# Layer 3 of a four-layer image kernel: where y is summed, the order of the scans, the last chunks' taps, and the places of the first loads

## The chip, the cores and the metric

The kernel runs on one core of one Trainium2 chip. TensorE (PE) multiplies matrices, VectorE (DVE), ScalarE (ACT) and GpSimd (POOL) work on 128 partitions at a time, and SyncE (SP) issues most of the DMAs. The metric is the time of one execution on the device in microseconds (us); lower is better. Profile times count from the start of the span.

## The reference, cut to what matters

The input x is (4, 64, 64, 128) in fp32: four images of 64 x 64 pixels and 128 channels. Four layers follow each other: a 7 x 7 neighbourhood attention, a full attention over the 4096 pixels of an image, a gated product with a row sum and a layer norm, and a selective scan in four directions. The change is in the last of these, which is

```python
xz = x @ Win
xb, z = jnp.split(xz, 2, axis=-1)                 # 256 channels each
xb = silu(depthwise_conv_3x3(xb) + conv_b)
xf, xt = xb as (B, 256, L), and with rows and columns exchanged
xs = stack([xf, xf[..., ::-1], xt, xt[..., ::-1]], axis=1).reshape(B * K, 256, L)
x_dbl = einsum('bcl,cd->bdl', xs, Wxproj)         # 8 numbers for delta, one B, one C
dt_kb = x_dbl[:, :8].reshape(K, B, 8, L)
delta = softplus(einsum('kdr,kbrl->bkdl', dt_weight, dt_kb) + dt_bias)
h[l]  = exp(delta[l] * A) * h[l - 1] + delta[l] * u[l] * B[l]
y[l]  = h[l] * C[l] + D * u[l]
y = y0 + y1 reversed + y2 turned + y3 reversed and turned
yz = y * silu(z);  out = layernorm(yz) @ Wout
```

The reshape from (B * K) to (K, B) mixes images and directions. So sixteen sequences are scanned for each of two halves of 128 channels. Source image k supplies its four directions b = 0 to 3 to the outputs of the four images: the scan (k, b) is added to output image b, plainly for k = 0 and 1, and with rows and columns exchanged for k = 2 and 3.

## The kernel before, in words

**Layers 0 to 2** (`layers_0_to_2`) run image by image. Within `layer_1(b)` a loop of 32 steps holds PE's long stretches of matmuls (L586, L619); at each step `between(i)` puts in one part of layer 2 (`turn`, `mix`, `add`, `norm`, for chunk n of 512 pixels from i = 6 + 4n) and one part of layer 3's front (`front(b)`), which lags half an image: chunks 4 to 7 of an image are done in the next image's loop. For the last image there is no next loop, and `end(i)` does them at i = 30 to 41.

**Layer 3's front**, for a chunk n of image i: `load` brings back x3, which `norm` had stored in DRAM (x3_d); `project` (L744) multiplies it by Win into xh, a tile with halo rows, which POOL copies from chunk to chunk; `gate` (L772) makes silu(z); `begin`, `multiply`, `add_parts` and `add_taps` compute the nine convolution taps on ACT, POOL (L813) and DVE (L822); `activate` (L764) makes u; `lower` (L833) makes D u, the dt, B and C rows (stored in dbl_d), and `times_b` (L868) stores u times B in ub_d. D u of the images 2m and 2m + 1 (the odd one reversed) is summed in DRAM:

```python
if i & 1:
    nc.gpsimd.dma_start(du_d[i >> 1][f][:, L - hi:L - lo], du, accum_op=ALU.add)
else:
    nc.sync.dma_start(du_d[i >> 1][f][:, lo:hi], du)
```

**Layer 3's scan stage** (`layer_3`) goes through 64 steps of `todo`; a step is two scans (two directions) of 128 channels x 1024 pixels. f (the channel half) is the outermost loop, then source image k, then the directions 0, 1 and 2, 3, with four chunks each. A step consists of: `deltas` (PE multiplies dbl by dt, L1144; ACT softplus, L1152, into de; POOL multiplies by ub into inp, L1154), issued one step ahead; `decay` (ACT exp into h in PSUM, L1164); `back` (DVE scan, L1178, its last column kept by L1181, and its product with C). For even k the product is written straight into y in SBUF (L1194). For odd k it goes to yo, a ring of 4 buffers (L1189), a POOL DMA adds it to y in SBUF (L1190), and SP stores y into y_d (L1192) unless it is the last pair (f, k) = (1, 3), whose y stays in SBUF. The load of a 2 MB row of C, broadcast to 128 partitions (`load_c`), comes 16 times, that of ub (`load_ub`, two halves of 1 MB) 8 times.

D u comes in beside this: `load_z` (L1103) loads the sums, `add_z` (L1105) adds the turned one on DVE (L1106, in steps 2 and 3) and stores the result as z_d, and from step 4 on POOL DMAs add z_d to y (L1211), two after each step.

**Layer 3's output stage** adds y and the turned y (`yts`, loaded by `load_turned`), multiplies by the gate, takes the norm and multiplies by Wout, in 32 chunks of 512 pixels.

**Order.** `tc.keep_in_program_order` pins some instructions on their engine (ACT in the scan stage, the whole output stage); the rest is ordered by the scheduler within each engine's queue. A ring (`tag`, `bufs`) makes a new tile wait for the release of the oldest. D u, u, silu(z), the sums of taps and others share the ring c512 of 9 tiles; the tag "ring" has 5 places of 16 KB per partition. POOL's DMAs signal through eight semaphores in turn, and so do SP's: the ninth waits until the first has landed.

Of the kernel before, what the change touches and what calls it, by code (L numbers as in the profile page):

```python
# [67 lines left out]
RC = CH // W  # L68

# [7 lines left out]
def conv_seq(ctx, tc, x, mata, matb, cols, rows, rpb, dtw, convw, sel, out):  # L77
# [13 lines left out]

    ub_d, zf_d = stored("ub_d"), stored("zf_d")
    du_d = [[dram.tile([P, L], F32, name=f"du_d{i}_{f}") for f in range(2)] for i in range(2)]
# [3 lines left out]
    fronts = x3_d, ub_d, zf_d, du_d, dbl_d, ct_d, gw_d, bw_d  # L97
# [9 lines left out]

    layers_0_to_2(tc, xf, mata, matb, rows, rpb, convw, sel, ident, cl, dram, *fronts)
    layer_3(tc, of, dtw, ident, cl, dram, *fronts)


@with_exitstack
def layers_0_to_2(
    ctx, tc, xf, mata, matb, rows, rpb, convw, sel, ident, cl, dram, x3_d, ub_d, zf_d, du_d, dbl_d, ct_d, gw_d, bw_d
# [3 lines left out]
    big = ctx.enter_context(tc.tile_pool(name="big", bufs=1))  # L118
# [20 lines left out]
    once = big.tile([P, NMA - nma + NROW - nrow], F32, name="once", tag="ring", bufs=5)  # L139
# [11 lines left out]

    def ring(shape, name):

        return big.tile(shape, F32, name=name, tag="ring", bufs=5)
# [497 lines left out]

    def layer_2(b, xt):
# [47 lines left out]
        def norm(n):  # L701
            mv, rd = kept.pop(n)
            for k in range(4):
                x = xt[:, 4 * n + k, :]
                nc.vector.tensor_scalar(x, x, mv[:, k, 0:1], rd[:, k:k + 1], ALU.subtract, ALU.mult)
            x3 = tmp.tile([P, CH], F32, name="x3", tag="c512", bufs=9)
            transpose_tiles(
                xt, 4 * n, x3,
                lambda o, i: nc.vector.tensor_scalar(
                    in_blocks(o), by_block(i, "r b c"), cl("ln_s"), cl("ln_b"), ALU.mult, ALU.add  # L710
                ),
            )
            nc.sync.dma_start(x3_d[b][:, bass.ts(n, CH)], x3)
# [12 lines left out]
    def front(b):  # L726
# [9 lines left out]
        def load(i, n):  # L736
            x = x_of[i, n] = tmp.tile([P, CH], F32, name="xc", tag="g1")
            nc.sync.dma_start(x, x3_d[i][:, bass.ts(n, CH)])
# [49 lines left out]
        def taps(i, n):  # L788


            v = (1, 0) if n < NCH - 1 else (-1, 0)
            gp, ve = [v, (-1, 1), (1, -1), (1, 1)], [(-v[0], 0), (0, -1), (0, 1), (-1, -1)]
            return (gp[:2], ve + gp[2:]) if at_end(i, n) else (gp, ve)

        def multiply(i, n, f, which):
            for k in which:
                dy, dx = taps(i, n)[0][k]
# [10 lines left out]
        def add_parts():  # L808
            for i, n, f, k, p in parts_of:
                of = taps(i, n)[0]  # L810
# [8 lines left out]
        def add_taps(i, n, f):  # L819
            for dy, dx in taps(i, n)[1]:  # L820
                acc, x, c = tap(n, f, dy, dx)
                nc.vector.scalar_tensor_tensor(acc, x, c, acc, ALU.mult, ALU.add)  # L822

        def activate(i, n, apart=False):
            if apart:
                u_of[i, n] = [tmp.tile([P, CH], F32, name="u1", tag="c512", bufs=9) for _ in range(2)]
                for f in range(2):
                    silu(i, n, u_of[i, n][f], accs[n & 1][:, f, :])
# [4 lines left out]
        def lower(i, n):  # L833

            lo, hi = CH * n, CH * n + CH
            u = u_of[i, n]
            for f in range(2):
                du = tmp.tile([P, CH], F32, name="du", tag="c512", bufs=9)
                nc.scalar.activation(du[:, ::-1] if i & 1 else du, u[f], AF.Copy, scale=cl("d", 2 * i + f))
                if i & 1:  # L840
                    nc.gpsimd.dma_start(du_d[i >> 1][f][:, L - hi:L - lo], du, accum_op=ALU.add)
                else:
                    nc.sync.dma_start(du_d[i >> 1][f][:, lo:hi], du)
# [70 lines left out]
        def convolve(i, n, fs, half):  # L914
            for f in fs:
                if half == 0:
                    begin(n, f)
                multiply(i, n, f, range(len(taps(i, n)[0]))[2 * half:2 * half + 2])
# [3 lines left out]
        def end(i):  # L922

            c = B - 1
            for n, at in ((5, 30), (6, 34), (7, 38)):
                if i == at:
                    load(c, n)
                if i == at + 1:
                    project(c, n)
                    for k in (n - 1, n)[0:1 + (n == NCH - 1)]:  # L930
                        convolve(c, k, range(2), 0)
                        convolve(c, k, range(2), 1)
                if i == at + 2:
                    gate(c, n)
            for n, at in ((4, 34), (5, 37), (6, 41), (7, 41)):
                if i == at:
                    activate(c, n, True)
                    lower(c, n)

        def turn(i):  # L940
# [33 lines left out]
            if b == 0 and i == 3:  # L974
                output_weights()
            if b == B - 1:
# [42 lines left out]
def layer_3(ctx, tc, of, dtw, ident, cl, dram, x3_d, ub_d, zf_d, du_d, dbl_d, ct_d, gw_d, bw_d):  # L1019
    nc = tc.nc  # L1020
    def pool(name, bufs=1, **kw):
# [4 lines left out]

    y_d = [
        [[dram.tile([P, L], F32, name=f"{name}{b}_{f}") for f in range(2)] for b in range(B)] for name in ("yn_d", "yt_d")  # L1030
    ]
    z_d = [dram.tile([P, L], F32, name=f"z_d{f}") for f in range(2)]
    bc_d = [[dbl_d[b][RANK:RANK + 1, :], dbl_d[b][RANK + 1:RANK + 2, :], ct_d[b]] for b in range(B)]


    dbl = wp.tile([P, L], F32, name="dbl")
    dt = wp.tile([P, DI], F32, name="dt")
    nc.sync.dma_start(dt, dtw)

    na = wp.tile([P, 2 * B], F32, name="na")  # L1040
    nc.scalar.activation(na, cl("a_log", n=2 * B), AF.Exp)
    nc.vector.tensor_scalar(na, na, -1.0, None, ALU.mult)
    gw = wp.tile([P, 2, C], F32, name="gw")
    bw = wp.tile([P, C], F32, name="bw")
    eps = wp.tile([P, 1], F32, name="eps")
    nc.vector.memset(eps, 1e-5)

    def by_rows(t):
        return t.rearrange("p (i j) -> p i j", j=W)


    ct = wp.tile([W, 2, W], F32, name="ct")

    def turn_c(b, pt):
# [4 lines left out]

    ub_s, cb_s = [wp.tile([P, L], F32, name="ub_0")], [wp.tile([P, L], F32, name="cb_0")]  # L1060

    def load_ub(tile, f, k):
        for g in range(2):
            half = bass.ts(g, L // 2)
            nc.sync.dma_start(tile[:, half], ub_d[k][f][:, half])

    def load_c(tile, k, t):

        nc.sync.dma_start(tile, bc_d[k][1 + t][0].partition_broadcast(P))
# [11 lines left out]
    for b in range(B):  # L1081
        nc.sync.dma_start(dbl[32 * b:32 * b + NDBL, :], dbl_d[b])
        if b == 1:
            load_ub(ub_s[0], 0, 0)
            load_c(cb_s[0], 0, 0)
# [5 lines left out]
    SC = 2 * CH  # L1091
    NSC = L // SC
    yp = ctx.enter_context(pool("y"))
    ub_s.append(yp.tile([P, L], F32, name="ub_1"))
    cb_s.append(yp.tile([P, L], F32, name="cb_1"))
    ys = [yp.tile([P, L], F32, name=f"y{b}") for b in reversed(range(B))][::-1]

    zs, zt = ys[2:4], ub_s[1]  # L1100

    def load_z(f, part):
        nc.sync.dma_start(zt if part else zs[f], du_d[part][f])  # L1103

    def add_z(f):  # L1105
        nc.vector.tensor_tensor(turned(zs[f]), turned(zs[f]), by_rows(zt), ALU.add)  # L1106
        for g in range(4):
            quarter = bass.ts(g, L // 4)
            nc.sync.dma_start(z_d[f][:, quarter], zs[f][:, quarter])

    for f, part in ((0, 0), (0, 1), (1, 0)):
        load_z(f, part)
    nc.sync.dma_start(gw, gw_d)
    nc.sync.dma_start(bw, bw_d)
    nc.sync.dma_start(ct[:, 0, :], by_rows(bc_d[B - 1][1])[0])
    with pool("s", 2) as sp, pool("psC", 2, space=PSUM) as psp:

        todo = []  # L1120
        fks = [(f, k) for f in range(2) for k in range(B)]
        for j, (f, k) in enumerate(fks):
            for half in range(2):
                loads = []
                if half == (j == 0) and j + 1 < len(fks):
                    loads.append((load_ub, ub_s[(j + 1) % 2], *fks[j + 1]))
                i = 2 * j + half + 1
                if i < 2 * len(fks):
                    loads.append((load_c, cb_s[i % 2], fks[i // 2][1], i & 1))
                for at_n in range(NSC):  # L1130
                    n = NSC - 1 - at_n if k & 1 else at_n
                    todo.append((loads, [(f, k, 2 * half + q, n, ub_s[j % 2], cb_s[half]) for q in range(2)]))
# [5 lines left out]
        def deltas(pair):  # L1138

            pdt = [psp.tile([P, 2, CH], F32, name=f"pdt{j}", tag=f"dt{j}", bufs=1) for j in range(2)]  # L1140
            for g in range(2):
                for j, (f, k, b, n, _, _) in enumerate(pair):
# [6 lines left out]
            for j, (f, k, b, n, ub, _) in enumerate(pair):  # L1149
                kf = 2 * k + f  # L1150
                de = sp.tile([P, SC], F32, name="de", tag="de", bufs=5)
                act(nc.scalar.activation(de, pdt[j].rearrange("p g t -> p (g t)"), AF.Softplus, bias=cl("dt_b", kf)))  # L1152
                inp = sp.tile([P, SC], F32, name="inp", tag="inp", bufs=4)
                nc.gpsimd.tensor_tensor(  # L1154
                    by_rows(inp), by_rows(de), at(ub, b ^ (k & 1), SC * n, SC * n + SC), ALU.mult
# [13 lines left out]
        def back(f, k, b, n, ub, cb, inp, h):  # L1169
# [9 lines left out]
            if n != last:  # L1179
                ends[b] = sp.tile([P, 1], F32, name="end", tag="end", bufs=4)  # L1180
                nc.vector.tensor_copy(ends[b], h[:, 0:1] if k & 1 else h[:, SC - 1:SC])  # L1181
            c = (cb[:, ::-1] if order & 1 else cb)[:, lo:hi]
            flip = slice(None, None, -1) if b & 1 else slice(None)
            if b & 1:
                lo, hi = L - hi, L - lo
            y = ys[b][:, lo:hi]
            if k & 1:
                yo = sp.tile([P, SC], F32, name="yo", tag="yo", bufs=4)
                nc.vector.tensor_tensor(yo[:, flip], h, c, ALU.mult)  # L1189
                nc.gpsimd.dma_start(y, yo, accum_op=ALU.add)  # L1190
                if (f, k) != (1, 3):
                    nc.sync.dma_start(y_d[k >> 1][b][f][:, lo:hi], y)  # L1192
            else:
                nc.vector.tensor_tensor(y[:, flip], h, c, ALU.mult)  # L1194
                if b >> 1 == k >> 1:
                    late.append((y, z_d[f][:, lo:hi]))
# [3 lines left out]
        for j, ((loads, pair), after) in enumerate(zip(todo, todo[1:] + [None])):  # L1200
# [3 lines left out]
            hs = [decay(step, de) for step, (de, _) in zip(pair, parts)]  # L1204
            for step, (_, inp), h in zip(pair, parts, hs):
                back(*step, inp, h)

            for _ in range(2 if j > 3 else 0):
                if late:
                    y, z = late.pop(0)  # L1210
                    nc.gpsimd.dma_start(y, z, accum_op=ALU.add)  # L1211
# [222 lines left out]
```

## Time and profile before

| | us |
|---|---|
| median of 3 runs | 3858.29 |
| lowest, highest | 3853.61, 3859.43 |
| profiled execution: its own time | 3861.6 |
| profiled execution: span | 3859.8 |
| PE, DVE, ACT, POOL busy | 3378.9, 2806.5, 2705.7, 1443.5 |
| mean granted clock of TensorE | 0.903 |

The span runs from the first to the last instruction in the trace; the execution's own time is 1.8 us longer. In the lists of groups, `out<-in` names the tiles, then the shapes and the count; behind the bars stand the busy time, the mean of one in ns, and the idle time of the engine just before them with what ended it. In the chain, each row is start, length, and what ran. PE and PEld are TensorE's matmuls and weight loads; an fp32 matmul is recorded as two passes.

### The profile page before, as it was taken

What the parts mean: (1) busy time and instruction counts of PE and PEld (TensorE: products, weight loads), DVE (VectorE), ACT (ScalarE), POOL (GpSimd) and SP (SyncE); (2) the same over time, 40 slices, a digit from 0 to 9 for tenths busy, and PEclk for the clock granted to TensorE, in tenths of its full rate; (3) what the DMA queues carried; (4) which work ended last, traced back from release to release, by engine and by line L of the source; (5) the groups of instructions that cost most, each with busy time, mean ns of one, the idle gap of its engine ahead of it and who ended that gap; (6) DMA issues with size and microseconds to landing.
All of it is one profiled execution on the core that took longest, in us unless ns stands there. A gap on an engine that the chain in (4) does not pass through costs nothing.

```text
span 3859.8 us, 69106 instructions
## 1 busy us (share of the span) xinstructions
PE 3378.9 (88%) x26676; PEld 2778.6 (72%) x26676; DVE 2806.5 (73%) x4855; ACT 2705.7 (70%) x4391; POOL 1443.5 (37%) x1556
## 2 busy tenths in 40 slices
PE   6999999999999999999999999999999944665647
PEld 4679989966799999668999995689999821222236
DVE  2667777856677878566778875667787848998968
ACT  3865667767677767676777676767776846998934
POOL 5510022244122222441223224412222346888866
PEclk7999999999999999999999999999999955555579
DMA  5100000121010112210111022100011176998998
GB/s 138 46 3 25 12 18 29 54 91 34 17 48 29 37 35 59 85 34 17 48 31 40 29 72 75 31 17 26 31 41 31 51 209 211 271 282 260 258 285 274
DMA packets 192525, 326.61 MB, mean 85 GB/s; under 512 B 22175, under 2 KB 110780, under 8 KB 185500
## 3 DMA queue, kind: packets, MB, share of 16 engines
q1 hardware_dynamic: 152900, 253.29, 19.1%
q0 software_dynamic: 19776, 60.17, 8.4%
q10 hardware_dynamic: 19520, 8.73, 0.8%
q8 instruction: 210, 3.44, 0.4%
q14 instruction: 119, 0.97, 0.1%
HBM read 178.17 MB, written 110.47 MB: 75 GB/s over the span
## 4 chain that ended last, share of the span: by engine, by line
PE 52%; DVE 20%; ACT 11%; issue 7%; DMA 6%; POOL 4%; SPq 1%; DVEq 0%; POOLq 0%; ACTq 0%
PE po L619 16%; PE sc L586 16%; DVE mx L598 4%; PE pt L470 3%; DVE mx L593 2%; POOL inp L1154 2%; PE sc L435 2%; PE po L481 2%; DVE acc L822 2%; DMA y<-yo 2%; DVE h L1178 2%; ACT pr L453 2%; ACT st L589 2%; ACT st L613 1%; PE pz L772 1%
## 5 line engine op out<-in xcount | busy, mean ns | idle before, releaser
L619 PE MATMUL po<-v,st 128*128 128x129 f32 x8192 | 1084.0, 275 | 4.1 <-ACT st L613 4.1
L586 PE MATMUL sc<-qT,kT 128*128 128x128 f32 x8192 | 1080.5, 276 | 0.4 <-ACT st L589 0.4
L586 PEld LDWEIGHTS sc<-qT,kT 128*128 128x128 f32 x8192 | 1001.0, 192 | 21.4 <-issue 18.6
L619 PEld LDWEIGHTS po<-v,st 128*128 128x128 f32 x8192 | 999.0, 192 | 5.8 <-issue 5.8
L589 ACT COPY st<-sc 128x512 f32<-128x512 f32 x1024 | 576.0, 583 | 496.9 <-PE sc L586 490.4
L612 DVE TENSOR_TENSOR st<-st,pb 128x2048 f32<-128x2048 f32 x256 | 574.0, 2283 | 46.9 <-PE pb L609 46.8
L613 ACT ACTIVATE st<-st 128x2048 f32<-128x2048 f32 x256 | 482.8, 1908 | 10.8 <-DVE st L612 9.3
L593 DVE TENSOR_TENSOR mx<-mx,st 128x1024 f32<-128x1024 f32 x256 | 314.2, 1227 | 235.5 <-ACT st L589 233.0
L1144 PE MATMUL pdt<-dbl,dt 8*128 8x512 f32 x512 | 308.5, 1088 | 194.6 <-ACT de L1152 186.4
L1154 POOL TENSOR_TENSOR inp<-de,ub 128x1024 f32<-128x1024 f32 x128 | 363.8, 2996 | 87.0 <-ACT de L1152 57.3
L1144 PEld LDWEIGHTS pdt<-dbl,dt 8*128 8x128 f32 x512 | 115.8, 314 | 384.6 <-ACT de L1152 314.4
L461 POOL TENSOR_SCALAR pr<-pr,sm 128x308 f32<-128x308 f32 (+3 forms) x512 | 243.4, 494 | 264.8 <-DVE sm L459 196.2
L681 POOL TENSOR_TENSOR x<-x,row 128x512 f32<-128x512 f32 x32 | 50.2, 1568 | 686.0 <-PE pt L253 686.0
L813 POOL TENSOR_TENSOR gsum<-gsum,tp 128x504 f32<-128x504 f32 (+1 forms) x176 | 246.0, 1399 | 152.5 <-ACT gsum L801 83.4
L453 ACT ACTIVATE pr<-pr,mx 128x308 f32<-128x308 f32 (+3 forms) x512 | 262.5, 517 | 0.0
L598 DVE TENSOR_TENSOR mx<-mx 128x512 f32<-128x512 f32 (+2 forms) x384 | 237.7, 619 | 6.0
L822 DVE SCALAR_TENSOR_TENSOR acc<-xh,cc,acc 128x504 f32<-128x504 f32 (+3 forms) x272 | 217.3, 832 | 17.8 <-ACT acc L786 16.9
L1178 DVE TENSOR_TENSOR_SCAN h<-h,end,inp 128x1024 f32<-128x1024 f32 x96 | 220.8, 2345 | 6.4 <-ACT h L1164 3.9
L470 PE MATMUL pt<-ident,pr 128*88 128x128 f32 (+5 forms) x1472 | 205.7, 277 | 7.8 <-ACT prT L472 7.8
L439 DVE CUSTOM_DVE_ANT_0 pr<-sc,bias_m 128x266 f32<-128x266 f32 (+1 forms) x384 | 151.7, 451 | 69.0 <-PE sc L435 65.3
L470 PEld LDWEIGHTS pt<-ident,pr 128*88 128x88 f32 (+5 forms) x1472 | 165.0, 139 | 45.5 <-ACT prT L472 31.6
L472 ACT COPY prT<-pt 110x512 f32<-110x512 f32 (+3 forms) x240 | 138.9, 579 | 77.8 <-PE pt L470 77.8
(225 smaller groups left out, 5230.4 us busy)
## 6 DMA issues: line engine op xcount, KB each, us to landing
y<-yo POOLq DMA_DIRECT2D x64, 512.0 KB, 12.6
zf_d<-zf SPq DMA_DIRECT2D x64, 256.0 KB
ub_d<-u SPq DMA_DIRECT2D x64, 256.0 KB
cb<-ct_d SPq DMA_DIRECT2D x8, 2048.0 KB
ub<-ub_d SPq DMA_DIRECT2D x16, 1024.0 KB
cb<-dbl_d SPq DMA_DIRECT2D x8, 2048.0 KB
y<-z_d POOLq DMA_DIRECT2D x32, 512.0 KB, 14.4
yn_d<-y SPq DMA_DIRECT2D x32, 512.0 KB
```

Of the source, the lines that this page charges most:

```text
L453: pin(nc.scalar.activation(k.pr[:, h], k.pr[:, h], AF.Exp, bias=k.mx[:, h:h + 1], accum_out=k.sm[:, h:h + 1]))
L470: pin(nc.tensor.transpose(pt[0:n, h, :], k.pr[:, h, at:at + n], ident))
L586: nc.tensor.matmul(ps[:, r, :], lhsT=kT[:, bass.ts(G * g + r, P)], rhs=qT[:, bass.ts(i, P)], start=True, stop=True)
L589: nc.scalar.copy(k.st[:, G * g:G * g + G, :], ps)
L593: nc.vector.tensor_tensor(k.mx, k.mx, k.st[:, 4 * g - 4:4 * g + 4, :], ALU.max)
L598: nc.vector.tensor_tensor(mx[:, 0:n, :], mx[:, 0:n, :], mx[:, n:2 * n, :], ALU.max)
L612: nc.vector.tensor_tensor(part, part, pb.unsqueeze(1).to_broadcast([P, 16, P]), ALU.add)
L613: nc.scalar.activation(part, part, AF.Exp)
L619: nc.tensor.matmul(k.po, lhsT=k.st[:, j, :], rhs=v[:, j, :], start=(j == 0), stop=(j == NT - 1))
L1144: nc.tensor.matmul(pdt[j][:, g, :], lhsT=dt[o:o + RANK, P * f:P * f + P], rhs=at(dbl[o:o + RANK, :], k & 2, g0, g0 + CH), start=True, stop ...
L1154: nc.gpsimd.tensor_tensor(by_rows(inp), by_rows(de), at(ub, b ^ (k & 1), SC * n, SC * n + SC), ALU.mult)
L1178: nc.vector.tensor_tensor_scan(h[:, way], h[:, way], inp[:, way], prev, ALU.mult, ALU.add)
```

## The change

1. **D u.** y_d becomes a set of DRAM tiles of 128 x 1024, for both halves f, both forms t (plain, turned) and all four images. `lower` writes D u straight into the four that it belongs to, by SP stores for even images and by POOL DMAs that add for odd ones: eight DMAs of 256 KB a chunk instead of two. `load_z`, `add_z`, z_d, du_d and L1211 are gone.
2. **y.** Every product of a scan goes through yo (ring of 6 instead of 4; de has 4 instead of 5) and is added by a POOL DMA: into y_d in DRAM, or, for (f, k) = (1, 3), into y in SBUF. For (f, k) = (1, 2) the product is written to y in SBUF, and the DRAM tile is added to it later, one DMA in each following step. The 48 stores of y are gone.
3. **Order of the scans.** k is the outermost loop; within it the parts are (f one, directions 0 and 1), (two, 0 and 1), (two, 2 and 3), (one, 2 and 3). A row of C then serves both halves, so there are 8 such loads instead of 16.
4. **Last image, chunks 4 to 7.** x3 stays in SBUF (x3k), without store and reload. The nine taps become nine TensorE matmuls into PSUM for each half f, with diagonal matrices of the coefficients, which POOL makes at i = 6 of the last image. The steps of `end` lie at other i.
5. **First loads.** dbl of images 0 and 1, ub and the row of C for the first steps are loaded at i = 32 of the last image, into the places of layer 1's qT and of the ring; y, the second row of C and others also take over layer 1's places. dt and na are made at the start of the kernel.
6. **Output.** The turned y is loaded in four pieces of 512 KB per image instead of two of 1 MB, and `yts` has another order.

```diff
+    na = const.tile([P, 2 * B], F32, name="na")
+    nc.scalar.activation(na, cl("a_log", n=2 * B), AF.Exp)
...
-            x3 = tmp.tile([P, CH], F32, name="x3", tag="c512", bufs=9)
+            stays = b == B - 1 and n >= 4
+            if stays:
+                x3 = fresh[n] = tmp.tile([P, CH], F32, name="x3k", tag="g1")
+            else:
+                x3 = tmp.tile([P, CH], F32, name="x3", tag="c512", bufs=9)
...
-            nc.sync.dma_start(x3_d[b][:, bass.ts(n, CH)], x3)
+            if not stays:
+                nc.sync.dma_start(x3_d[b][:, bass.ts(n, CH)], x3)
...
+        def diagonals():
+            dg = x_of["dg"] = ring([P, 2, 9, P], "dg")
+            for f in range(2):
+                for t in range(9):
+                    nc.gpsimd.tensor_scalar(dg[:, f, t, :], ident, cc[:, f, t:t + 1], None, ALU.mult)
+
+        def convolve_by_pe(i, n):
+            sums[n] = []
+            for f in range(2):
+                ps = ps_s([P, CH], "pc3")
+                order = [(0, 0)] + [(dy, dx) for dy in (-1, 0, 1) for dx in (-1, 0, 1) if (dy, dx) != (0, 0)]
+                for k, (dy, dx) in enumerate(order):
+                    r0, r1, c0, c1 = region(n, dy, dx)
+                    nc.tensor.matmul(
+                        by_image_rows(ps)[:, r0:r1, c0:c1], lhsT=x_of["dg"][:, f, 3 * (dy + 1) + dx + 1, :],
+                        rhs=xh[:, n & 1, f, 1 + r0 + dy:1 + r1 + dy, c0 + dx:c1 + dx], start=(k == 0), stop=(k == 8),
+                    )
+                sums[n].append(ps)
...
+            at = L - hi if i & 1 else lo
             for f in range(2):
                 du = tmp.tile([P, CH], F32, name="du", tag="c512", bufs=9)
                 nc.scalar.activation(du[:, ::-1] if i & 1 else du, u[f], AF.Copy, scale=cl("d", 2 * i + f))
-                if i & 1:
-                    nc.gpsimd.dma_start(du_d[i >> 1][f][:, L - hi:L - lo], du, accum_op=ALU.add)
-                else:
-                    nc.sync.dma_start(du_d[i >> 1][f][:, lo:hi], du)
+                for b2 in range(B):
+                    to = y_d[(i ^ b2) >> 1][b2][f][at // SC][:, at % SC:at % SC + CH]
+                    if i & 1:
+                        nc.gpsimd.dma_start(to, du, accum_op=ALU.add)
+                    else:
+                        nc.sync.dma_start(to, du)
...
             for n, at in ((5, 30), (6, 34), (7, 38)):
                 if i == at:
                     load(c, n)
-                if i == at + 1:
                     project(c, n)
-                    for k in (n - 1, n)[0:1 + (n == NCH - 1)]:
-                        convolve(c, k, range(2), 0)
-                        convolve(c, k, range(2), 1)
-                if i == at + 2:
                     gate(c, n)
-            for n, at in ((4, 34), (5, 37), (6, 41), (7, 41)):
+            for n, at in ((4, 33), (5, 34), (6, 38), (7, 38)):
                 if i == at:
+                    convolve_by_pe(c, n)
                     activate(c, n, True)
+            for n, at in ((4, 34), (5, 35), (6, 39), (7, 39)):
+                if i == at:
                     lower(c, n)
+            if i == NT:
+                early.ub = big.tile([P, L], F32, name="ub_0", tag="qT")
+                early.dbl, early.cb = ring([P, L], "dbl"), ring([P, L], "cb_0")
...
-    def add_z(f):
-        nc.vector.tensor_tensor(turned(zs[f]), turned(zs[f]), by_rows(zt), ALU.add)
-        for g in range(4):
-            quarter = bass.ts(g, L // 4)
-            nc.sync.dma_start(z_d[f][:, quarter], zs[f][:, quarter])
...
+        for k in range(B):
+            one, two = k & 1, 1 - (k & 1)
+            for part, f in enumerate((one, two, two, one)):
...
-            y = ys[b][:, lo:hi]
-            if k & 1:
-                yo = sp.tile([P, SC], F32, name="yo", tag="yo", bufs=4)
+            m = NSC - 1 - n if b & 1 else n
+            there, here = y_d[k >> 1][b][f][m], ys[b][:, SC * m:SC * m + SC]
+            if f == 1 and k == 2:
+                nc.vector.tensor_tensor(here[:, flip], h, c, ALU.mult)
+                late.append((here, there))
+            else:
+                yo = sp.tile([P, SC], F32, name="yo", tag="yo", bufs=6)
                 nc.vector.tensor_tensor(yo[:, flip], h, c, ALU.mult)
-                nc.gpsimd.dma_start(y, yo, accum_op=ALU.add)
-                if (f, k) != (1, 3):
-                    nc.sync.dma_start(y_d[k >> 1][b][f][:, lo:hi], y)
-            else:
-                nc.vector.tensor_tensor(y[:, flip], h, c, ALU.mult)
-                if b >> 1 == k >> 1:
-                    late.append((y, z_d[f][:, lo:hi]))
+                nc.gpsimd.dma_start(here if f == 1 and k == 3 else there, yo, accum_op=ALU.add)
```

## The prediction

> **What bounds the kernel now.** I read the page's slices first, then busy times by window, then the groups, the waits and the chain of the last 960 us. The slices (40 equal parts of 96.5 us) show two kernels in one:
>
> ```profile
> PE   6999999999999999999999999999999944665647
> DVE  2667777856677878566778875667787848998968
> POOL 5510022244122222441223224412222346888866
> PEclk7999999999999999999999999999999955555579
> DMA  5100000121010112210111022100011176998998
> ```
>
> Up to slice 32 TensorE is the bound and DMA is nearly idle; the last eight slices are layer 3, where DVE, POOL and DMA are full and the granted clock is 0.5. All that the change can win lies there. The last matmul of layer 1 (L619) ends at 3086.1, the first scan starts at 3181.6, the last scan product is done at 3696.1. That makes three stages: a handover of 95.5 us, a scan stage of 514.5, and an output stage of 163.5. The windows (sum over the window of PE, PEld, DVE, ACT, POOL busy us, then clock, DMA share, GB/s):
>
> ```profile
> 3050.00:3100.00 50.00, 42.03 (x333) 35.52 (x333) 39.68 (x64) 37.57 (x50) 18.99 (x18) 0.91 0.35 86
> 3100.00:3150.00 50.00, 19.63 (x76) 9.81 (x75) 29.76 (x42) 23.51 (x37) 22.15 (x19) 0.64 0.62 201
> 3300.00:3400.00 100.00, 64.68 (x108) 23.58 (x107) 94.31 (x75) 94.45 (x83) 89.73 (x49) 0.50 0.97 279
> 3400.00:3500.00 100.00, 56.52 (x96) 21.00 (x94) 80.22 (x66) 79.87 (x71) 81.48 (x46) 0.50 1.05 288
> ```
>
> No engine is full in the handover: it is one chain of dependences. In the scan stage's good window DVE and ACT are 94% busy and DMA is at 0.97; in the next one DMA is at 1.05 and the engines fall to 80%, so there they wait for transfers. The groups and waits of the scan stage:
>
> ```profile
> L1178 DVE TENSOR_TENSOR_SCAN h<-h,end,inp 128x1024 f32<-128x1024 f32 x96 | 220.8, 2345 | 6.4 <-ACT h L1164 3.9
> L1189 DVE TENSOR_TENSOR yo<-h,cb 128x1024 f32<-128x1024 f32 x64 | 77.2, 1216 | 19.0 <-DMA y<-yo 19.0
> L1194 DVE TENSOR_TENSOR y<-h,cb 128x1024 f32<-128x1024 f32 x64 | 76.7, 1216 | 22.7 <-DMA yt_d<-y 12.1 <-DMA z_d<-y 10.7
> L1190 POOL DMA_DIRECT2D y<-yo x64 | 66.2, 1137 | 26.8 <-DVE yo L1189 22.4 <-DVE end L1181 1.9 <-ACT h L1164 1.3
> L1106 DVE TENSOR_TENSOR y<-y,ub 128x4096 f32<-128x4096 f32 x2 | 21.5, 10727 | 0.0
> ```
>
> A step is two scans; undisturbed steps start 7.03 us apart. ACT's part of one is two Softplus, two Exp and the two table loads between them: 2 x 1.110 + 2 x 1.117 + 2 x 1.283 = 7.02 (means of L1152, L1164 and their loads), which sets that step. DVE's, 2 x (2.345 + 1.216 + 0.150) = 7.4 by records that overlap, stands level. So 63 steps and a last one of 7.3 need 450 us, and 64 of the 514.5 are stalls. The rows account for them: add_z itself 21.5, y waiting for z_d's stores 10.7, y waiting for yt_d's stores 12.1, yo waiting for its accumulate 19.0; sum 63.3. The chain has the same pieces, and the handover's before them:
>
> ```profile
> 3118.23 11.13 DMA x_d<-x
> 3129.42 2.89 DMA xc<-x_d
> 3137.71 13.79 DVE acc L822 x12
> 3159.38 8.25 issue
> 3229.58 10.51 DVE y L1106
> 3241.03 14.67 DMA z_d<-y
> 3466.96 30.30 DMA yt_d<-y
> ```
>
> **Scan stage.** add_z, z_d and the y_d stores are gone: -21.5 - 10.7 - 12.1 = -44.3, with no successor on DVE. The yo waits (19.0) remain in kind: 112 products now go through yo instead of 64, which at the same rate would be 19.0 x 112/64 = 33, but the ring has 6 buffers, three steps (21 us), where 4 gave 14 us against a median landing of 12.6 (largest 17.6 by the trace's records). I take 13 of waits left: -44.3 - 19 + 13 = **-50**. The ends: 3 left gives -60; 33 left, -30.
>
> What is late next is POOL or DMA. POOL issues two accumulates in nearly every step (112 + 16 late ones, against 64 + 32 before), median 0.88 us, mean 1.14; where turned products (2.85 us each) and two issues met before, its period was 6.8 us by the trace's records, just below the step; the 16 late ones are a third issue in their steps, within the 13. DMA: the software queue moved 60.17 MB in 8.4% of the span, 5.4 us of all 16 engines per MB, and a step now has 1 MB of it. The loads, 14 of 2 MB at the hardware queue's 2.9 us per MB, add 1.3 a step: 6.7 of 7.03. But before all of the stage's accumulates added in SBUF (4 KB packets, 0.327 us each); now 96 of 128 add in DRAM. The nearest rows are the 32 du_d accumulates, 2 KB packets at a median of 0.178 and means of 0.208 to 0.240, so 0.36 to 0.48 for 4 KB. At 0.36 the step has 5.8 + 1.3 = 7.1 against the 7.03 x 1.05 = 7.4 that the share of 1.05 shows to be possible. I take the median, as the means hold a few long first packets: covered, barely.
>
> The same row has the landing: 6.2 us for 256 KB added in DRAM, 12.6 for 512 KB added in SBUF, no sign of a dearer target. The Trainium skill ("DMA: Bandwidth & Descriptors", Anatomy of one DMA) speaks against the change: a DMA's fixed cost of about 2 us is mostly the write receipt, and DRAM's is the heaviest. By that rule I estimate 14.6 us a landing, still under the ring's 21, and the sum stays.
>
> **Handover.** Gone from the chain: store and reload of x3 (14.0), DVE's last taps (13.8), the reload of dbl at its end (the 8.25 of issue). Added: (1) Taps of chunks 4 and 5 stand on PE ahead of layer 2's last mix. A tap matmul has 512 columns in two passes; four passes of pz take 1.72 us at full clock, 0.43 each, so 18 taps take 15.5 us a chunk. With the projections between, PE reaches the last mix near 3126, the last x3 is ready near 3144, and pi of chunk 7 starts at 3148 (before 3132). (2) 36 taps of chunks 6 and 7 follow: 31 us, u of chunk 7 at 3183. (3) lower of chunks 6 and 7 issues 16 accumulates on POOL, and the first inp of the scans stands behind them in POOL's order. Eight issues take 8 x 1.0 us (du_d row: median 0.999); as the program gives POOL's DMAs eight semaphores, the ninth waits for the first's landing. At 5.4 us per MB 256 KB is 1.4 us, 16 of them 22: POOL is free at 3200 to 3206, and the next step's inp, whose buffers lie over du's, at 3210 to 3216. The scans start as if at 3203 to 3211 against 3181.6: I take **+24**. Below: +10, if landings do not queue. Above: +50.
>
> That upper end is the clock. In the handover pi takes a mean of 0.843 us a pass and pz 0.756, and the granted clock goes 0.91, 0.64, 0.50; at 0.843 the last 36 taps take 61 us instead of 31, +30. I take the full clock, since 36 taps in a row load PE as layer 1 did (96.9 of 100 us busy from 2900 to 3000, clock 1.00). The Trainium skill ("TensorE: Matmul & The Clock Gate", Part 1) has full clock after about 3.4 us of sustained work; by it I would estimate +2 where the row gives +30, though the scan windows with PE 65% busy and a clock of 0.50 show that not all work counts as sustained.
>
> **Layers before.** lower issues four DMAs where it issued one: 96 more accumulates (96 x 0.999 = 96 us on POOL) and 96 more stores (median 0.343, 33 us of SP's queue). Queued behind them are POOL's halo copies, tap sums and L681, and SP's loads of xc and bb; du's buffer in the ring of 9 is held by four landings. POOL is 27% busy in the window from 2900, PE 97%, so the cover is large: **+2**, 0 to +15. If it failed by 1 us in each of 16 odd chunks, that is the upper end. The 18 diagonals (some 0.5 us each, as POOL's L461) and the early loads, at a DMA share of 0.1 to 0.35, cost nothing; gone cover would show them as a wait of the first step, at most 2 MB x 2.9 us.
>
> **Output stage.** The first turned loads were already issued ahead of it; 512 KB pieces let them start a little sooner at a share of 0.93: **-3** (-8 to +2).
>
> Sum: -50 + 24 + 2 - 3 = -27. The profiled execution took 3861.6 (span 3859.8 and 1.8 around it), 3.3 over the median of 3858.29; the same 27 off the median is 3831.
>
> **Rivals.** *Accumulates in DRAM bound the scan stage (slower).* If a 4 KB packet takes c us, a step needs 16c + 1.3 at a share of 1.05. It passes 7.03 at c = 0.38, and at c = 0.42 the step is 7.65 and the whole change is even. At 0.45 it is 8.1: 64 x 8.1 = 518, +4 on the stage, and 4 + 24 + 2 - 3 = +27: 3885. For: the means of du_d's packets. Against: their median, and a queue that is full amortises first packets. *Taps at half clock.* -27 + 30 = +3: 3861, no change. For: the pi and pz rows. Against: the chain of taps has no gaps. *Handover hidden, ring enough.* -60 + 10 - 3 = -53: 3805. For: 21 us of ring against a landing of 12.6. Against: a DMA share near 0.95 leaves bursts nowhere to go.
>
> **How the numbers follow.** About 0.2% (7.7 us) can be told from no change here. Forecast 0.48 (own range 3811 to 3851), DRAM bound 0.18, half clock 0.16, hidden 0.18. Faster: 0.42 + 0.18 + 0.03 of the half-clock case, 0.63. Slower: 0.17 + 0.07 + 0.02, 0.26. Same: 0.11. The range goes from under the hidden case to near the DRAM-bound one, 3796 to 3880.
>
> **What would show it.** Right: scan steps at 7.0 with some 13 us of yo waits, first scan near 3205, the last 36 taps in about 31 us, no idle PE before 3086. Wrong: steps above 7.3 with DMA near 1.05 and packets over 0.38 us; taps at 0.85 a pass; POOL's accumulates of du still issuing after 3210; the last L619 matmul later than 3095.

## The result: slower by 0.36%, and the profile after

The changed kernel takes 3869.98 us (median of 10 runs) against 3856.76 (median of 10 runs of the kernel before): ratio 1.0036, 95% interval 1.0026 to 1.0046. The forecast was 27 us faster; the measured change is 13.2 us slower. The median is inside the range of 3796 to 3880, but the change is on the other side of zero.

The four stages, taken from each trace in the same way (end of the last matmul of layer 1; start of the first scan; start of the last scan product; end of the span). The prediction's 514.5 and 163.5 go by the end of that product, 1.2 us later. Here and in the table of the experiments, times agree with the profile's rows to 0.3 us:

| | predicted change | before | after | change |
|---|---|---|---|---|
| layers 0 to 2, last matmul of layer 1 at | +2 | 3086.1 | 3121.8 | **+35.7** |
| handover, to the first scan | +24 | 95.5 | 119.3 | +23.8 |
| scan stage | -50 | 513.4 | 460.5 | -52.9 |
| output stage | -3 | 164.8 | 167.0 | +2.2 |
| span | -27 | 3859.8 | 3868.5 | +8.7 |

The spans differ by 8.7 us and the medians by 13.2, because the profiled execution of the kernel before took 4.8 us more than its median; the changes of the stages sum to some 5 us too little.

Three of the four terms came out within 6 us. The one that was called covered, "POOL is 27% busy in the window from 2900, PE 97%, so the cover is large", lost 35.7 us. The slices of the changed kernel's page hide it, because PE still shows nines; only POOL's row has more in it in the middle:

```profile
PE   6999999989999999898999998989999987666647
DVE  2657777856677778466777885667778725999968
POOL 5510022245122233451232323513213336999966
PEclk8999999999999999899999999999999996555569
DMA  5100001231011123410222213101112187999998
```

The windows of the handover and the scan stage (PE, PEld, DVE, ACT, POOL busy, clock, DMA share, GB/s) show the part that went as planned:

```profile
3100.00:3150.00 50.00, 50.00 (x268) 31.99 (x267) 15.69 (x33) 21.38 (x30) 22.03 (x24) 1.00 1.01 271
3150.00:3200.00 50.00, 39.22 (x134) 19.48 (x133) 7.44 (x22) 12.68 (x19) 15.71 (x19) 0.86 0.59 120
3400.00:3500.00 100.00, 68.63 (x118) 25.79 (x115) 98.56 (x79) 98.41 (x86) 99.33 (x58) 0.50 1.00 227
```

DVE and ACT are at 98% where they were at 80% before (94% in the better window), and the step is 7.0 us. In the handover the granted clock is 0.89 from 3121 to 3182 and 1.00 from 3182 to 3212; before, it fell to 0.64 and 0.50. The groups of the scan stage (3180 to 3720):

```profile
L1206 DVE TENSOR_TENSOR_SCAN h<-h,end,inp 128x1024 f32<-128x1024 f32 x96 | 221.2, 2346 | 14.7 <-POOL inp L1182 6.8 <-ACT h L1192 4.3
L1220 DVE TENSOR_TENSOR yo<-h,cb 128x1024 f32<-128x1024 f32 x112 | 133.9, 1212 | 1.7 <-DMA y<-yo 1.7
L1221 POOL DMA_DIRECT2D y<-yo x112 | 222.6, 3087 | 6.0 <-DVE yo L1220 3.8 <-DVE end L1209 2.0 <-issue 0.2
```

The waits of yo are 1.7 us (19.0 before, 13 foretold). add_z and the waits for z_d and yt_d are gone.

**Where the 35.7 us went.** Matching each of the 16384 matmuls of layer 1's loops with its partner before gives the delay at the start and end of each image's loop: image 0: +0.8, +0.9; image 1: +4.8, +10.0; image 2: +20.4, +22.8; image 3: +25.6, +35.7. So three places lose time: the stretch between the loops of images 1 and 2 (10.4), the loops themselves (17.7 in images 1 to 3, most in image 3 with 10.1 and image 1 with 5.2), and the ends of the even images 0 and 2 (3.9 and 2.8).

*Between images 1 and 2.* Between two loops PE has only the last chunks of layer 2 and the start of the next layer 0, and there it depends on POOL. POOL's timeline at that place, with PE's row for that mix behind it, after and then before (start, length, idle time before with its releaser):

```profile
1554.49 7.10 POOL L897 DMA_DIRECT2D y<-du  x8 [0.91 <-ACT du L893]
1575.69 2.48 POOL L926 TENSOR_TENSOR u<-u,bb 128x512 f32<-128x512 f32 x2 [12.81 <-DMA bb<-dbl_d]
1578.13 1.05 POOL L700 TENSOR_TENSOR o<-o,rt 128x512 f32<-128x512 f32 x1
1579.23 2.08 PE L711 MATMUL py<-ma,o 128*128 128x128 f32 x8 [14.89 <-POOL o L700]
```

```profile
1544.62 1.76 POOL L841 DMA_DIRECT2D du_d<-du  x2 [4.76 <-ACT du L839]
1556.41 2.48 POOL L870 TENSOR_TENSOR u<-u,bb 128x512 f32<-128x512 f32 x2 [7.62 <-DMA bb<-dbl_d]
1558.85 1.05 POOL L677 TENSOR_TENSOR o<-o,rt 128x512 f32<-128x512 f32 x1
1559.96 2.08 PE L688 MATMUL py<-ma,o 128*128 128x128 f32 x8 [5.54 <-POOL o L677]
```

POOL is not busy: it stands 12.8 us in front of u times B (7.6 before), because bb is not there, and behind that instruction waits o, layer 2's last mix, for which PE waits: 14.9 us instead of 5.5, so 9.4 of the 10.4. SP's timeline shows why bb is late, again after and then before:

```profile
1560.27 1.95 SPq L910 DMA_DIRECT2D dbl_d<-dq  x4
1572.22 0.34 SPq L922 DMA_DIRECT2D bb<-dbl_d  x1
```

```profile
1547.12 2.98 SPq L854 DMA_DIRECT2D dbl_d<-dq  x4
1552.91 0.34 SPq L866 DMA_DIRECT2D bb<-dbl_d  x1
```

bb's load waits for dbl_d's four stores of 5 KB to land. Between the end of their issue and the load lie 10.0 us (1572.22 - 1562.22) instead of 2.8. Sixteen accumulates of 256 KB were issued just before them, from 1539.4 on. They were not all that stood ahead: in SP's own queue stand two loads of layer 0's bias tiles (bias_m, 1.18 MB), the first issued 1.8 us before the stores, where the kernel before has 5.1. The records of DMA packets have the bias loads from 1561.8 to 1568.9 and the stores' packets from 1569.6 to 1571.6. In e6 below, with bias loads 2.8 us ahead of the stores and no accumulate, the gap is 3.7 us. So the 10.0 comes from the accumulates and the bias loads together; a run with these accumulates and no bias loads ahead was not made.

Two of the 28 loads of bb have a gap of 10.0. The other begins at 3125.3, after layer 1's last matmul, and is no part of the 35.7 us.

*In the loops* it is another wait. PE waits there for DVE's maximum of the scores (mx): 38.2 us in the four loops before, 56.7 after, a difference of about the size of what the loops lose. The longest of these waits is in image 3. PE's row for it, and a part of the maximum ahead of it on DVE, after and then before:

```profile
3069.06 0.47 PE L624 MATMUL pt<-ident,mx 128*128 128x128 f32 x1 [5.13 <-DVE mx L619]
3054.57 4.29 DVE L612 TENSOR_TENSOR mx<-st 128x1024 f32<-128x1024 f32 x1
```

```profile
3035.79 0.33 PE L603 MATMUL pt<-ident,mx 128*128 128x128 f32 x1 [1.31 <-DVE mx L598]
3025.13 1.21 DVE L591 TENSOR_TENSOR mx<-st 128x1024 f32<-128x1024 f32 x1
```

In both kernels such a part of the maximum takes at most 1.23 us when no POOL instruction runs beside it. Beside POOL's work it takes up to 2.3 us before and up to 4.3 after. At this place POOL has just issued eight accumulates (7.1 us from 3048.1 on), and its products and additions follow in one piece until 3068.9. That this bunching holds DVE up fits the times; no run moved POOL's additions alone.

### The profile page after: what moved, and what is told of

Its sections match the earlier page's. It is cut to its first block, busy times and chain, and to the rows that moved or that the text cites. A ratio compares the mean times of both kernels' runs of the same rounds, so it can differ in the third digit from the quotient of the medians.

```text
span 3868.5 us, 69546 instructions
## 1 busy us (share of the span) xinstructions
PE 3426.0 (89%) x26820; PEld 2798.9 (72%) x26820; DVE 2761.5 (71%) x4805; ACT 2687.9 (69%) x4365; POOL 1541.3 (40%) x1686
## 3 DMA queue, kind: packets, MB, share of 16 engines
q0 software_dynamic: 38208, 102.12, 14.9%
## 5 line engine op out<-in xcount | busy, mean ns | idle before, releaser
L610 ACT COPY st<-sc 128x512 f32<-128x512 f32 x1024 | 576.1, 583 | 512.7 <-PE sc L607 506.1
L614 DVE TENSOR_TENSOR mx<-mx,st 128x1024 f32<-128x1024 f32 x256 | 329.3, 1286 | 242.6 <-ACT st L610 240.0
L1182 POOL TENSOR_TENSOR inp<-de,ub 128x1024 f32<-128x1024 f32 x128 | 416.6, 4712 | 6.6 <-ACT de L1178 3.2
L842 POOL TENSOR_TENSOR gsum<-gsum,tp 128x504 f32<-128x504 f32 (+1 forms) x168 | 262.9, 1625 | 136.7 <-ACT gsum L830 77.3
L1221 POOL DMA_DIRECT2D y<-yo x112 | 222.6, 3087 | 6.0 <-DVE yo L1220 3.8
L491 PEld LDWEIGHTS pt<-ident,pr 128*88 128x88 f32 (+5 forms) x1472 | 163.6, 138 | 45.6 <-ACT prT L493 31.6
## 6 DMA issues: line engine op xcount, KB each, us to landing
y<-du POOLq DMA_DIRECT2D x128, 256.0 KB, 10.1
```

Source lines behind the costliest of these rows:

```text
L491: pin(nc.tensor.transpose(pt[0:n, h, :], k.pr[:, h, at:at + n], ident))
L610: nc.scalar.copy(k.st[:, G * g:G * g + G, :], ps)
L614: nc.vector.tensor_tensor(k.mx, k.mx, k.st[:, 4 * g - 4:4 * g + 4, :], ALU.max)
L842: nc.gpsimd.tensor_tensor(a, a, p, ALU.add)
L1182: nc.gpsimd.tensor_tensor(by_rows(inp), by_rows(de), at(ub_s[f], b ^ (k & 1), SC * n, SC * n + SC), ALU.mult)
L1221: nc.gpsimd.dma_start(here if f == 1 and k == 3 else there, yo, accum_op=ALU.add)
```

## The experiments

Theory A: the accumulates of `lower` hold up the ends of the images, through POOL's queue and through the small transfers of dbl_d behind them. Theory B: another part of the change costs the 36 us (even images' stores, diagonals, kept x3, early loads). The stage columns of all runs stand in one table at the end of this section.

**e1, e2: fewer accumulates, or none.** In e1 an odd image's D u goes to one of its four tiles:

```diff
-                for b2 in range(B):
+                for b2 in range(1 if i & 1 else B):
```

> Of the changed kernel, the odd images' D u goes to one of its four y tiles instead of all four (three of four additions are left out; even images' stores stay): 32 accumulates of 256 KB instead of 128. Theory A (the accumulates of lower hold up POOL's queue and the small transfers of dbl_d behind them at the ends of the images): the last matmul of layer 1 ends near 3092 instead of 3121.8 (30 of the 35.7 us lost there come back), the handover to the first scan falls from 119 to about 103, the scan stage stays at 460, about 3825 in all. Theory B (the loss comes from the rest of the change: diagonals, early loads, x3 kept, even stores): the last matmul stays above 3110, and the total above 3850.

In e2 it goes to all four, plainly:

```diff
-                    if i & 1:
-                        nc.gpsimd.dma_start(to, du, accum_op=ALU.add)
-                    else:
-                        nc.sync.dma_start(to, du)
+                    nc.sync.dma_start(to, du)
```

> Of the changed kernel, the odd images' D u is stored plainly by SP instead of added by POOL (the sum of the two images is left out): the same 256 transfers of 256 KB, none on POOL. Theory A in its POOL form (POOL's queue is the place): as e1, last matmul near 3092, about 3825. Theory A in its transfer form (the bytes ahead of dbl_d's small stores are the place): a plain transfer takes about half of an accumulate's time, so half of the loss stays: last matmul near 3105, about 3843. Theory B: above 3110 and above 3850.

Measured: last matmul at 3095.6 and 3092.6; 3829.15 us (ratio 0.9936, 0.9921 to 0.9950) and 3832.92 (0.9947, 0.9932 to 0.9961). With the accumulates 26 and 29 of the 35.7 us are gone, and the longest gap before a load of bb is 4.8 and 5.3. Theory A stands; B holds at most the remaining 6 to 9. The delays of e1 say where those are: 3.6 and 4.9 us at the ends of images 0 and 2, under 1.3 in any loop. These are even images, whose D u is stored by SP, eight stores of 256 KB ahead of dbl_d's. The handover shortens too, by 14 and 9. The bytes by themselves did little: e2 moves as many as the changed kernel.

**e5: only the order.** D u's eight DMAs are issued after u has been multiplied by B:

```diff
                     times_b(*c, x_of.pop((*c, "b")), nc.gpsimd)
+                    give_du(c[0], x_of.pop((*c, "du")))
```

> Of the changed kernel, only the order in lower is altered: D u is computed as before, but its eight DMAs per chunk are issued after u has been multiplied by B, so dbl_d's stores and bb's load go ahead of them; the number and kind of DMAs and POOL's work stay. If the place of the loss is the wait for bb behind the accumulates' transfers (POOL's multiplication by bb, and layer 2's sums behind it in POOL's queue), the last matmul of layer 1 ends near 3100 instead of 3121.8, about 3848 in all. If it is POOL's own time for issuing 128 accumulates (some 7 us a chunk of an odd image), it stays above 3112 and the total above 3860.

Measured: 3105.9, halfway, and 3853.99 us in one run. The delays from image to image say which half: at the ends of images 0 and 2, +3.9 and +2.8 became -2.5 and -1.5, and there only even images' stores moved, so this much of the loss was theirs; the loop of image 1 still loses 5.0 (5.2 in the changed kernel), that of image 3 loses 6.3 instead of 10.1, and between images 1 and 2 10.2 us stay. There chunk 3's dbl_d still finds the accumulates of chunk 2, issued from 1545.5 on, and the bias loads ahead of it, and its gap is 9.9. So both readings hold a part: the place of the DMAs in the order, and the accumulates themselves.

**e3, e6, e9: the same sum without accumulates.** An even image stores D u once; an odd one loads that chunk, adds, and stores the sum to the four tiles. In e3 DVE adds; in e6 POOL does, in the loops; in both the part stands behind bb's load:

```diff
+            nc.sync.dma_start(du, y_d[i >> 1][0][f][at // SC][:, at % SC:at % SC + CH])   # in activate
...
+            nc.vector.scalar_tensor_tensor(du[:, ::-1], u[f], cl("d", 2 * i + f), du[:, ::-1], ALU.mult, ALU.add)   # e3
+            nc.scalar.activation(du[:, ::-1], u[f], AF.Copy, scale=cl("d", 2 * i + f))   # e6
+            nc.gpsimd.tensor_tensor(du, du, pre, ALU.add)
+            for b2 in range(B if i & 1 else 1):
+                nc.sync.dma_start(y_d[(i ^ b2) >> 1][b2][f][at // SC][:, at % SC:at % SC + CH], du)
```

> The whole computation, D u summed another way: an even image stores D u once, an odd image loads that chunk, DVE adds its own D u in one instruction, and SP stores the sum plainly to the four tiles, after dbl_d and bb are under way. No accumulate before the scans, 32 + 128 stores and 32 loads instead of 256 stores and accumulates. Theory A: last matmul near 3092 (32 DVE instructions of 0.75 us in layer 1's loop may cost some us), handover near 100 since POOL is free for the first inp, scan stage 460: about 3822, faster than both kernels. Theory B: last matmul above 3110, total above 3850.

> As e3, but in the loops the addition of the even image's D u is made by POOL (two of 1.25 us a chunk) on ACT's D u, and by DVE only in the last image's chunks 4 to 7. If e3 lost its 36 us because its DVE instructions and their wait for the loaded chunk stand in DVE's queue in front of layer 1's softmax work, the last matmul ends near 3093; handover 102, scan stage 461: about 3826, faster than both kernels by 0.7%. If the loaded chunk's wait is the loss on whichever engine, it stays above 3108.

Both missed. The last matmul stayed at 3122.1 and 3121.8 although no accumulate was left; 3853.45 (1.0006, 0.9996 to 1.0016) and 3852.82 (0.9999, 0.9990 to 1.0009), level with before because the handover is 18 and 16 us shorter than in the changed kernel. The delays had another shape: nothing is lost between the images, but each loop from image 1's on loses 10 to 15 us (image 0's 2.5), mostly in pieces of 2 to 3 after a call of lower, for even images too. In e6, PE's waits for DVE's maximum sum to 72.8 us in the four loops, against 38.2 before. It is another loss of about the same size, which these versions brought in themselves. ACT's timeline of e6 has D u directly ahead of the copies of scores (st, L610) that DVE's maximum reads; at the same place e9, the next run, has the copies at once:

```profile
1136.66 0.30 ACT L720 ACTIVATE rd<-mv,eps 128x4 f32<-128x4 f32 x1
1136.87 1.32 ACT L908 ACTIVATE du<-u,col 128x512 f32<-128x512 f32 x2
1138.09 1.05 ACT L610 COPY st<-sc 128x512 f32<-128x512 f32 x2
```

```profile
1131.97 0.30 ACT L720 ACTIVATE rd<-mv,eps 128x4 f32<-128x4 f32 x1
1132.18 1.05 ACT L610 COPY st<-sc 128x512 f32<-128x512 f32 x2
```

e9 makes D u ahead of dq's copy again, as the changed kernel does, and is otherwise e6:

```diff
+            make_du(i, n)          # ACT's D u and POOL's addition, before pd
             pd = ps_t([P, P], "pd")
...
             nc.sync.dma_start(bb, dbl_d[i][RANK:RANK + 1, lo:hi][0].partition_broadcast(P))
+            give_du(i, n)          # the stores
```

> As e6, with one thing moved: ACT makes D u ahead of its copy of dq (the dt, B and C rows), as the changed kernel does, and POOL adds the loaded chunk there; the stores stay after bb's load. e3 and e6 lost 2 to 3 us of PE's time after every call of lower, for even images too, which neither the loaded chunk nor the engine that adds it explains. If that was ACT standing idle for dq's matmul with D u's two instructions behind it, the last matmul of layer 1 ends near 3090 instead of 3121.8 and the total is near 3822, 0.8% faster than the kernel before. If it was the loaded chunks or the stores after bb, the last matmul stays above 3110 and the total above 3840.

Measured: last matmul at 3087.0, within 1 us of the kernel before; **3818.75 us, ratio 0.9906 (0.9889 to 0.9922), faster than both kernels**. At the place shown above, e9's wait for bb is:

```profile
POOL u L950 <- DMA bb<-dbl_d: 5.5, 1, 5.5
PEld py L711 <- POOL o L700: 4.2, 1, 4.2
```

against 12.8 and 15.8 in the changed kernel. So the diagonals, the kept x3 and the early loads, all still in e9, cost at most the 4.3 us that image 3's loop loses in it. The even images' stores are not cleared by it: e9 has one of them where the changed kernel has four, behind bb's load. And the level is a sum: by the delays e9 loses 11.5 us in the loops, most in image 2's, and gains 10.4 between them. Of e6's loss it is shown that moving D u in ACT's order, with the addition that follows it, ends it; whether ACT's bubble at dq or the place ahead of st is the larger part was not told apart.

**e4, e7: part 4 undone.** The last chunks' taps are on ACT, POOL and DVE again, and x3 goes through DRAM; e4 is the changed kernel, e7 is e6.

```diff
-            for n, at in ((4, 33), (5, 34), (6, 38), (7, 38)):
+            for n, at in ((4, 34), (5, 37), (6, 41), (7, 41)):
                 if i == at:
-                    convolve_by_pe(c, n)
                     activate(c, n, True)
```

> Of the changed kernel, part 4 undone: the last image's chunks 4 to 7 have their taps on ACT, POOL and DVE again, x3 goes through DRAM, and the steps of end are the old ones; all else as changed. If TensorE's taps shorten the handover, it grows from 119 to about 135, and the total from 3870 to about 3885. If they cost time (36 of them stand before layer 2's last mix), it falls to about 110 and the total to about 3860. The last matmul of layer 1 (3121.8) moves by less than 5 either way if the loss before it is lower's, and back by 9 if the diagonals and kept x3 make the last image's part of it.

> e6 with part 4 undone (taps of the last chunks on ACT, POOL and DVE, as in e4). e4 gained 14 us in the handover and 3 before it, and gave 9 back in the first step, where inp waited for the landing of D u's accumulates; without accumulates that wait has no cause. Last matmul near 3091, handover near 92, scan stage 462: about 3813. If the taps on TensorE are the better way once POOL is free, it is above e6 by some us.

e4: last matmul 3118.6, handover 105.2, but 9 us back in a first step of 16.6; 3859.75 us, ratio 1.0016 (1.0006 to 1.0026) where the changed kernel has 1.0036. e7 equals e6 (3852.83 against 3852.82), so its expectation missed like e6's, and its handover is 105.4, not 92. Without accumulates part 4 was worth nothing (e6 and e7); beside them it cost 8 us by these ratios.

**e8, e10: the ring, and the early loads.** One run of each. e8 also gives de its five buffers back.

```diff
-                yo = sp.tile([P, SC], F32, name="yo", tag="yo", bufs=6)
+                yo = sp.tile([P, SC], F32, name="yo", tag="yo", bufs=4)
```

> Of the changed kernel, the ring of yo has 4 buffers and that of de 5, as in the kernel before; all else as changed. The prediction said that four would leave 33 us of waits of yo in the scan stage and six some 13: then the scan stage is 480 instead of 460.5, and the total about 3890. If the accumulates into DRAM land soon enough for four (14 us), the stage stays within 5 us.

> Of the changed kernel, part 5's early loads undone: dbl of images 0 and 1, the first ub and the first row of C are loaded at the start of layer 3 (same places), after the last chunk's stores. The prediction put 8.25 us of the old handover on the reload of dbl. If the early loads are worth that, the handover grows from 119 to about 128, and the total to about 3878; if the accumulates on POOL are later than the loads anyway, it stays within 2 us.

e8: the scan stage grows to 476.0 (480 foretold), by the waits that the group of yo now shows (1.7 with six buffers):

```profile
L1220 DVE TENSOR_TENSOR yo<-h,cb 128x1024 f32<-128x1024 f32 x112 | 134.2, 1215 | 23.0 <-DMA y<-yo 23.0
```

Its handover grew by 10 as well: POOL's first inp waits 10.0 us for the landing of D u's last accumulate, where in the changed kernel it follows the issue at once (3238.2) and only the fourth waits, 2.7 us. Why the first one waits in e8 is not shown. e10 stays within 1 us: the early loads were hidden behind what was later still.

| | last matmul | handover | scan stage | output | median us |
|---|---|---|---|---|---|
| e1 one tile | 3095.6 | 105.0 | 460.3 | 166.7 | 3829.15 |
| e2 plain | 3092.6 | 110.5 | 461.0 | 165.9 | 3832.92 |
| e3 DVE adds | 3122.1 | 101.7 | 460.7 | 165.5 | 3853.45 |
| e4 taps back | 3118.6 | 105.2 | 469.2 | 165.9 | 3859.75 |
| e5 order | 3105.9 | 119.6 | 461.8 | 164.9 | 3853.99 (one run) |
| e6 POOL adds | 3121.8 | 103.6 | 459.0 | 166.7 | 3852.82 |
| e7 e6, taps back | 3120.0 | 105.4 | 459.0 | 167.0 | 3852.83 |
| e8 ring of 4 | 3120.8 | 129.2 | 476.0 | 163.6 | 3891.47 (one run) |
| e9 D u first | 3087.0 | 101.9 | 460.4 | 167.4 | 3818.75 |
| e10 late loads | 3121.5 | 120.3 | 461.6 | 165.5 | 3870.74 (one run) |

The kernel before was run again beside each group: 3851.45 us beside e1 to e4, 3851.39 beside e5 to e8, 3853.10 beside e9 and e10, but 3856.76 beside the changed kernel. The ratios go by these; medians of different groups compare to some 5 us.

## Why the prediction was wrong, step by step

**Layers before: the step that failed.** The prediction counted 96 accumulates at 0.999 us, named what is queued behind them (even bb), and then priced them by POOL's busy share in a window inside a loop. That share says nothing about what is late when. At the ends of the images a chain without slack runs through POOL: stores of dbl_d, load of bb, u times B, o, PE. After image 1 the cost was not POOL's time but a landing: 10.0 us instead of 2.8 for stores of 5 KB, behind 16 accumulates and the bias loads. In the loops, 17.7 us went where PE waited longer for DVE's maximum, while POOL's work stood in one piece behind eight issues. At the ends of the even images 6.7 went to SP's added stores ("33 us of SP's queue"), which the prediction counted as covered. At "1 us in each of 16 odd chunks" the upper bound was 15; the runs show 26 to 29 us for the accumulates (e1, e2), and 35 when D u is summed otherwise and stored behind bb's load (e9). The prediction's own sign of this, a last matmul of layer 1 later than 3095, came true.

**Handover: right in sum, +24 against +23.8.** The pieces also held: 36 taps in 29.95 us against 31, the first inp behind the last accumulate's issue (3237.7), and the second step's second inp behind its landing:

```profile
3182.33 29.95 PE pc L867 x72
3237.66 10.50 DMA y<-du
3248.38 2.35 POOL inp L1182
```

The half-clock rival is answered by the granted clock of 1.00 from 3182 to 3212, where these taps ran. pi's and pz's rows misled because they came from a stretch with gaps (PE busy 19.63 of 50 us). The rule of the Trainium skill ("TensorE: Matmul & The Clock Gate", Part 1), by which the prediction had estimated +2, was the better guide here.

**Scan stage: right, -50 against -52.9**, with 1.7 us of yo's waits where 13 were left. The rival of DRAM-bound accumulates did not come: it needed 4 KB packets of over 0.38 us, and they took 0.328 at the median and 0.360 on average (0.327 and 0.337 before, all of them into SBUF). The software queue as a whole moved 102.12 MB in 14.9% of the span, 5.6 us per MB against 5.4 before. The median landing of yo's accumulate fell from 12.6 to 11.0 us. The Trainium skill ("DMA: Bandwidth & Descriptors", Anatomy of one DMA) had led to an estimate of 14.6; no dearer landing of DRAM is seen, though other transfers beside it changed too.

**Output stage: wrong by 5 us.** The first load of yl starts at 3698.0, 3.4 us before the last product, where it started 11.4 before it; the places that it waits for were not looked into.

The slower rival was given 0.26 in all, for causes that did not act; what acted, the lost cover of lower's DMAs, had been priced at 15 at most and given no case of its own.

## What to carry to other kernels

A share of busy time in the middle of a loop does not show that added work is covered: look for the chain at each end of the loop, ask of every DMA that is added which small transfer, with someone waiting for it, will land behind it, and ask which work is pushed together behind its issue. Issue the small transfer that others wait for first, and sum on an engine with slack instead of by many accumulating DMAs; but check where the moved instructions then stand in each engine's order, since moving two ACT instructions of 0.7 us, with the addition behind them, took or gave 35 us here (e6 and e9).

## What the runs showed of the hardware that was not expected

POOL's DMA issues and its multiplications overlap in the records: in the scan stage the mean of an inp is 4.7 us (3.0 before) and that of an issue 3.1 (1.1 before), two of each in a step of 7.0 us, while the step does not grow and POOL's busy time is 99.33 of 100. A long POOL record behind several DMA issues is no measure of what the instruction costs:

```profile
L1182 POOL TENSOR_TENSOR inp<-de,ub 128x1024 f32<-128x1024 f32 x128 | 416.6, 4712 | 6.6 <-ACT de L1178 3.2 <-DMA y<-du 2.7
```
